# Scores of layer 1's first attention in PSUM groups of three banks instead of two

## The chip, the cores and the metric

The kernel runs on one core of a Trainium2 chip, as one launch. The metric is device time in microseconds (us) of that launch; lower is better. Engines are named as the profile names them: PE is TensorE (PEld its weight loads), ACT is ScalarE, DVE is VectorE, POOL is GpSimd, SP the queue that issues most DMAs. A PSUM bank holds 512 fp32 numbers in each of 128 partitions, and this part of the kernel uses all eight banks.

## The reference

Four layers, each an attention and a feed-forward part, on four sequences of 1024 tokens of width 128. The change touches only the first attention of layer 1. Cut to that:

```
mean = jnp.mean(sequence, axis=-1, keepdims=True)
var  = jnp.mean(jnp.square(sequence - mean), axis=-1, keepdims=True)
x = (sequence - mean) / jnp.sqrt(var + EPS) * ln_gamma + ln_beta
q = _split_heads(x @ Wq.T + bq)          # 16 heads of 8
k = _split_heads(x @ Wk.T + bk)
v = _split_heads(x @ Wv.T + bv)
scores = jnp.einsum('bhqd,bhkd->bhqk', q, k) / scale
scores = jax.nn.sigmoid(scores - mu) * jnp.exp(scores)
scores = scores / jnp.sum(scores, axis=-1, keepdims=True)
out = jnp.einsum('bhqk,bhkd->bhqd', scores, v)
return out @ Wo.T + bo
```

Every score therefore goes through ScalarE twice, once as sigmoid and once as exp, and through VectorE once, for their product. The sum over keys comes out of the value product itself, since a column of ones stands beside the values.

## The kernel before

`_attention1` (line 652) works through 16 pairs n of a sequence b and a group g of four heads. The queries of a pair are taken in two halves of 512 (`qh`), so that the stage has 32 equal **halves**. Keys lie on the partitions, 128 at a time (`kc`, 0 to 7), queries on the free axis. The four heads of a group lie on partitions 0, 32, 64 and 96 of the query and key tiles, so the score matmuls of four heads use four different row strips of TensorE. One score tile of one head and one block of keys, 128 keys by 512 queries, is one bank; a half has 32 of them, here called **units**.

A half is made of two **passes** over the same 32 units, because sigmoid and exp need different tables in ScalarE:

- In the first pass (x from 0 to 7) PE computes the scores of two units (line 723) into a `big` PSUM tile of two banks, and one ACTIVATE over 128 x 1024 numbers (line 734) turns them into a tile `p` in SBUF.
- In the second pass (x from 8 to 15) PE computes the same scores again, one ACTIVATE with the other function (line 738) makes a tile `e`, and VectorE multiplies `p` by `e` in place (line 740).

The order of the two functions alternates from half to half (`turn`), so that one table load per half is enough. Sigmoid takes its bias from a column in SBUF (`neg_mu`), exp takes a constant.

`weigh` is the value product of one block of keys: four matmuls (line 418, in `_weigh`), one per head, that add to the one-bank tile `av`. They are put into a list `waiting` and taken out of it by hand: one per x, only while x is below `LAG` = 3 or from 8 + `LAG` on. So blocks 0 to 4 are weighed at x = 11 to 15, and blocks 5 to 7 at x = 0 to 2 of the next half. After block 7 VectorE copies `av` out (line 757) and hands `_normalise` (four transposes into the bank `misc`, a reciprocal and a product) to the background work.

Background work is a queue of generators, `later`, of which one step is taken at every x, after the two groups of that x. Besides `_normalise` it holds `_project_out` (for each sequence two rounds of four transposes, line 449, and one output matmul, line 455), and `prepare`, which makes queries, keys and values of the next sequence while the present one is worked on. It is added at the first half of g = 1, three times in all. Its 17 steps are: a load; four times a projection (PE matmul line 376, VectorE line 378, then ScalarE line 388 one step later, then VectorE line 390 and the DMAs to DRAM one step later); four times two value matmuls (line 408) and one VectorE addition (line 411). Projection and value matmuls take their PSUM tiles from the same `big` pool as the scores, in the same rotation.

The engines PE, DVE and ACT run in program order here (`manual_schedule`): an instruction that waits holds up all that stand behind it on its engine. The buffers are: `big` three tiles of two banks, `misc` and `av` one bank each, `p` 18 tiles of 1024 numbers, `e` four.

Of the kernel before, what the change touches and what calls it, by code (L numbers as in the profile page):

```python
# [10 lines left out]
F32 = mybir.dt.float32  # L11
# [208 lines left out]
def _bc(ap, axis, n):  # L220

    ap = ap.unsqueeze(axis)
    shape = list(ap.shape)
    shape[axis] = n
    return ap.to_broadcast(shape)
# [139 lines left out]
def _project_halves(k, wts, biases, rotary, xin, hl, ps, w, adder=None):  # L365

    nc = k.nc
    for part in range(2):  # L370
        for h in range(2):
            own = slice(h * W, (h + 1) * W)
            x = w.tile([P, W], F32, name="px")
            t = ps()
            for n, wt in enumerate(wts[part]):
                nc.tensor.matmul(t[:, n, :], wt, xin[:, own], start=True, stop=True)
            if rotary is None:
                nc.vector.tensor_scalar(x, t[:, 0, :], biases[part][0], None, ALU.add)
            else:
                r = [w.tile([P, W], F32, name=f"rot{n}") for n in range(2)]  # L380
                for n in range(2):
                    nc.vector.scalar_tensor_tensor(
                        r[n], t[:, n, :], biases[part][n], rotary[:, n, own], ALU.add, ALU.mult
                    )
                adder.tensor_tensor(x, r[0], r[1], ALU.add)
            yield
            hi, lo = w.tile([P, W], R, name="phi"), w.tile([P, W], R, name="plo")
            nc.scalar.copy(hi, x)
            yield
            nc.vector.tensor_tensor(lo, x, hi.bitcast(F32), ALU.subtract)  # L390
            for n in range(4):
                half = (lo if n // 2 else hi) if part == 0 else (lo if n % 2 else hi)
                nc.sync.dma_start(hl[part][:, n, :, own], half.bitcast(F32))
            yield
# [7 lines left out]
def _values(k, xin, wv, bv, v, ps):  # L402

    nc = k.nc
    for t in range(0, 8, 2):
        vp = ps()
        for m in range(2):
            nc.tensor.matmul(
                vp[:, m, :VW], xin[:, (t + m) * P : (t + m + 1) * P], wv, start=True, stop=True
            )  # L410
        nc.vector.tensor_tensor(v[:, t : t + 2, :], vp[:, :, :VW], _bc(bv, 1, 2), ALU.add)
        yield
# [239 lines left out]
def _attention1(k, a):  # L652
    nc, tc = k.nc, k.tc
    LAG = 3
    with ExitStack() as s:
        pool = lambda name, bufs, **kw: s.enter_context(tc.tile_pool(name=name, bufs=bufs, **kw))
        wp = pool("w1", 1)
        wqk, wv, wo = k.load(wp, a["l1_wqk"]), k.load(wp, a["l1_wv"]), k.load(wp, a["l1_wo"])
        bv = wp.tile([P, VW], F32, name="bv1")
        nc.sync.dma_start(bv, a["l1_bv"].to_broadcast([P, VW]))  # L660
        neg_mu = wp.tile([P, 1], F32, name="neg_mu")
        nc.vector.tensor_scalar(neg_mu, k.vec("l1_mu"), -1.0, None, ALU.mult)
        wts = [[wqk[:, m * P : (m + 1) * P]] for m in range(2)]
        biases = [[k.vec("l1_b" + x)] for x in "qk"]
        xp, vp, op, w = pool("xl", 1), pool("v", 2), pool("o", 2), pool("aw", 2)
        hp, pp, ep = pool("heads", 2), pool("p", 18), pool("e", 4)
        big = pool("big", 3, space=PSUM)
        misc = pool("misc", 1, space=PSUM)
        avp = pool("av", 1, space=PSUM)
        two = lambda: big.tile([P, 2, W], F32, name="big")  # L670
        one = lambda: misc.tile([P, W], F32, name="misc")
        heads, values = {}, {}

        def prepare(b):
            xl = xp.tile([P, L], F32, name="xl")
            nc.sync.dma_start(xl, k.xl[b])
            values[b] = vp.tile([P, 8, VW], F32, name="v")
            yield
            yield from _project_halves(k, wts, biases, None, xl, k.hl[b], two, w)
            yield from _values(k, xl, wv, bv, values[b], two)  # L680

        def load(n):
            q, key = hp.tile([P, L], R, name="q32"), hp.tile([P, L], R, name="k32")
            for part, dst in ((1, key), (0, q)):
                src = _to_heads(k.hl[n // 4][part], n % 4)
                nc.sync.dma_start(dst.bitcast(F32), src.rearrange("h r t -> (h r) t"))
            heads[n] = q, key

        scale = 8.0**-0.5
        funcs = [(AF.Sigmoid, neg_mu), (AF.Exp, 0.0)]  # L690
        later = _Steps()
        for _ in prepare(0):
            pass
        load(0)
        s.enter_context(tc.manual_schedule(engines=ENGINES))
        o = None
        turn = 0
        waiting = []
        for n in range(16):
            b, g = divmod(n, 4)  # L700
            if g == 0:
                o = op.tile([P, 8, D], F32, name="o")
            if g == 1 and b + 1 < B:
                ready = prepare(b + 1)
                later.add(ready)
            if g == 3 and b + 1 < B:
                later.until(ready)
            if n + 1 < 16:
                load(n + 1)
            q, key = heads.pop(n)  # L710
            v = values[b]
            for qh in range(2):


                first = {}
                av = None
                for x in range(16):
                    kc = x % 8
                    for pair in range(2):
                        ps = two()  # L720
                        for jj in range(2):
                            rows = slice(32 * (2 * pair + jj), 32 * (2 * pair + jj) + 32)
                            nc.tensor.matmul(  # L723
                                ps[:, jj, :],
                                key[rows, kc * P : (kc + 1) * P],
                                q[rows, qh * W : (qh + 1) * W],
                                start=True,
                                stop=True,
                                tile_position=(32 * (2 * pair + jj), 0),
                            )  # L730
                        f, bias = funcs[turn]
                        if x < 8:
                            p = pp.tile([P, 2, W], F32, name="p")
                            nc.scalar.activation(p, ps, f, bias=bias, scale=scale)  # L734
                            first[kc, pair] = p
                        else:
                            e = ep.tile([P, 2, W], F32, name="e")
                            nc.scalar.activation(e, ps, f, bias=bias, scale=scale)  # L738
                            p = first[kc, pair]
                            nc.vector.tensor_tensor(p, p, e, ALU.mult)  # L740
                        if pair == 0 and waiting and (x < LAG or x >= 8 + LAG):
                            waiting.pop(0)()
                    later.step()
                    if x == 7:
                        turn ^= 1
                    if x < 8:
                        continue
                    if av is None:
                        av = avp.tile([P, W], F32, name="av")

                    def weigh(av=av, v=v, b=b, g=g, qh=qh, kc=kc, first=first, o=o):
                        pts = [first[kc, j // 2][:, j % 2, :] for j in range(4)]
                        _weigh(k, v, g, kc, pts, av, slice(0, W))
                        if kc < 7:
                            return
                        osb = w.tile([P, W], F32, name="osb")
                        nc.vector.tensor_copy(osb, av)
                        later.add(_normalise(k, osb, o[:, 4 * qh : 4 * qh + 4], g, one, w))
                        if g == 3 and qh == 1:
                            copy = nc.vector.tensor_copy  # L760
                            later.add(
                                _project_out(k, b, o, wo, k.vec("l1_bo"), k.x, one, w, copy)
                            )

                    waiting.append(weigh)
        while waiting:
            waiting.pop(0)()
        later.finish()


# [1451 lines left out]
```

## Time and profile before

| what | value |
|---|---|
| median of 3 runs | 4753.9 us (4752.63 to 4770.15) |
| the profiled execution's own time | 4760.07 us |
| its span | 4758.3 us |
| mean granted clock of PE in it | 0.862 |
| first score matmul and last `weigh` of the stage | 1376.4 us and 2483.3 us from the span's start |
| ACT busy over the span | 2562.6 us (54%) |
| PE busy over the span | 3887.6 us (82%) |
| DVE busy over the span | 3111.6 us (65%) |
| ACT busy from 1378 to 2486 us | 1047.59 of 1108 us |
| DVE busy there | 654.56 us |
| PE busy there, and its granted clock | 938.82 us, 0.74 |

The profile is one execution. Its page lists busy time per engine, then the span in 40 slices of 119 us with the busy share of each engine in tenths, then DMA, the chain of work that ended last, and groups of instructions by source line, with their count, busy time, mean duration and the idle time of the engine just before them. A view by time merges runs of equal instructions: start, length, engine, line, what it writes and reads, the count, and in square brackets the idle time before it and who ended it. A mean duration is longer than the time from one start to the next, since ACT and DVE begin an instruction before the last one's write is acknowledged.

### The profile page before, as it was taken

To read this page: it belongs to the slowest core of one execution; us is meant where nothing else is said; L and a number is where in the kernel's file an instruction comes from. 1 tells how busy PE (TensorE), PEld (TensorE's weight loads), DVE (VectorE), ACT (ScalarE), POOL (GpSimd) and SP (SyncE) were. 2 spreads that over 40 slices of the span, in tenths; PEclk is the share of its full clock that TensorE was granted. 3 is DMA by queue.
4 is the path that set the end of the run, shared out by engine and by line. 5 is a ranking of instruction groups with operands and counts; after the bars stand their busy time and mean duration, and the time that the engine had idled before them with its cause. 6 is when DMAs were issued, how large, how long until landed. Compare 5 with 4: busy or idle time off the path is not lost. (4 is left out here: it accounts for less than half of the span.)

```text
span 4758.3 us, 54361 instructions
## 1 busy us (share of the span) xinstructions
PE 3887.6 (82%) x20924; PEld 1774.2 (37%) x20924; DVE 3111.6 (65%) x4404; ACT 2562.6 (54%) x3611; POOL 649.7 (14%) x639
## 2 busy tenths in 40 slices
PE   4679999998968888888877888888879966888564
PEld 3223333364332222222224555555534543333221
DVE  5868989722336656565657888888465323899876
ACT  1257877831259999999984555455422112344331
POOL 1310000003100000000003232233103122000132
PEclk6689999999967777777778999999889987999788
DMA  2411121021221010100002111111100223300001
GB/s 86 118 41 55 29 59 26 11 72 49 14 83 58 18 49 18 36 27 18 18 13 65 36 41 35 40 34 32 37 0 23 63 64 83 97 0 9 0 0 53
DMA packets 107494, 191.81 MB, mean 40 GB/s; under 512 B 23138, under 2 KB 48354, under 8 KB 105378
## 3 DMA queue, kind: packets, MB, share of 16 engines
q1 hardware_dynamic: 98756, 166.31, 12.3%
q0 software_dynamic: 8192, 16.79, 1.7%
q10 hardware_dynamic: 288, 5.24, 0.3%
q8 instruction: 165, 2.70, 0.2%
q14 instruction: 93, 0.76, 0.1%
HBM read 95.00 MB, written 67.39 MB: 34 GB/s over the span
## 5 line engine op out<-in xcount | busy, mean ns | idle before, releaser
L740 DVE TENSOR_TENSOR p<-p,e 128x1024 f32<-128x1024 f32 x512 | 586.7, 1221 | 321.7 <-ACT e L738 321.7
L723 PE MATMUL big<-q,k 32*128 32x512 f32 x2048 | 560.3, 633 | 180.6 <-ACT p L734 74.9
L533 DVE TENSOR_REDUCE m<-mx 128x2 f32<-128x1024 f32 x512 | 620.9, 1223 | 101.4 <-PE mx L525 94.2
L418 PE MATMUL av<-p,v 128*32 128x256 f32 (+1 forms) x5632 | 666.4, 528 | 0.3
L616 ACT ACTIVATE p<-s 128x512 f32<-128x512 f32 x1024 | 550.9, 597 | 184.7 <-PE s L607 171.5
L723 PEld LDWEIGHTS big<-q,k 32*128 32x128 f32 x2048 | 210.8, 229 | 707.0 <-ACT e L738 347.3
L607 PE MATMUL s<-q,k 64*128 64x512 f32 x1024 | 277.7, 494 | 48.4 <-DMA q<-mrows 33.4
L738 ACT ACTIVATE e<-big,neg_mu 128x1024 f32<-128x1024 f32 x256 | 262.0, 1125 | 11.7 <-PE big L723 11.4
L525 PE MATMUL mx<-k,q 64*128 64x512 f32 x1024 | 238.8, 437 | 32.3 <-DVE m L533 17.8
L734 ACT ACTIVATE p<-big,neg_mu 128x1024 f32<-128x1024 f32 x256 | 261.2, 1199 | 3.0 <-PE big L723 2.8
L738 ACT ACTIVATE e<-big 128x1024 f32<-128x1024 f32 x256 | 243.0, 1040 | 28.8 <-PE big L723 27.2
L734 ACT ACTIVATE p<-big 128x1024 f32<-128x1024 f32 x256 | 239.4, 1076 | 8.2 <-PE big L723 8.1
L1177 POOL TENSOR_TENSOR lqk<-lt 128x512 f32<-128x512 f32 x128 | 162.5, 1269 | 518.1 <-DVE lt L1168 461.3
L1150 PE MATMUL lps<-f_wqkv,lh 128*128 128x512 f32 x384 | 215.2, 649 | 11.7 <-DVE lo L1305 6.8
L1871 PE MATMUL sm<-hist,in_const_sb 128*128 128x512 f32 x252 | 144.0, 701 | 93.1 <-ACT hist L1896 79.5
L1031 POOL DMA_INDIRECT cl_row<-res,back x128 | 121.2, 947 | 713.7 <-DMA in_l_su_sb<-in_l_su 474.3
L418 PEld LDWEIGHTS av<-p,v 128*32 128x32 f32 x5632 | 121.3, 111 | 253.1 <-issue 202.6
L607 PEld LDWEIGHTS s<-q,k 64*128 64x128 f32 x1024 | 107.5, 184 | 284.9 <-issue 162.3
L1268 ACT ACTIVATE lsm<-lsm 128x512 f32<-128x512 f32 x128 | 80.6, 630 | 222.1 <-DVE lsm L1267 220.7
L1896 ACT COPY hist<-sm 128x992 f32<-128x992 f32 (+1 forms) x65 | 64.9, 999 | 224.0 <-DVE pro L1879 143.4
L950 POOL DMA_INDIRECT buf<-xtok,to x128 | 125.9, 983 | 407.7 <-DMA buf<-xtok,to 221.3
L1143 POOL MEMSET lva<- 128x32 f32 x16 | 2.4, 152 | 1148.1 <-PE av L418 1148.1
(412 smaller groups left out, 6888.5 us busy)
## 6 DMA issues: line engine op xcount, KB each, us to landing
hl<-phi SPq DMA_DIRECT2D x64, 256.0 KB, 2.9
hl<-plo SPq DMA_DIRECT2D x64, 256.0 KB, 3.5
lvs<-lva SPq DMA_DIRECT2D x16, 520.0 KB, 5.7
q<-hl SPq DMA_DIRECT2D x32, 256.0 KB, 5.2
k<-hl SPq DMA_DIRECT2D x32, 256.0 KB, 5.9
q<-hl SPq DMA_DIRECT2D x16, 512.0 KB, 5.3
k<-hl SPq DMA_DIRECT2D x16, 512.0 KB, 3.5
lvs<-lva SPq DMA_DIRECT2D x16, 390.0 KB
```

The lines of the kernel that those rows point to most:

```text
L418: k.nc.tensor.matmul(av[32 * j : 32 * j + 32, cols], v[:, kc, 9 * (4 * g + j) : 9 * (4 * g + j) + 32], pts[j][:, cols], start=kc == 0, sto ...
L525: nc.tensor.matmul(ps[:, i, :], q[rows, gg, qt * P : (qt + 1) * P], key[rows, gg, half * W : (half + 1) * W], start=True, stop=True, tile_ ...
L533: nc.vector.tensor_reduce(m[:, qt, gg, :, half], ps, AX.X, ALU.max)
L607: nc.tensor.matmul(ps, key[rows, half, kc * P : (kc + 1) * P], q[rows, half, qh * W : (qh + 1) * W], start=True, stop=True, tile_position= ...
L616: nc.scalar.activation(p, ps, AF.Exp, scale=8.0**-0.5)
L723: nc.tensor.matmul(ps[:, jj, :], key[rows, kc * P : (kc + 1) * P], q[rows, qh * W : (qh + 1) * W], start=True, stop=True, tile_position=(3 ...
L734: nc.scalar.activation(p, ps, f, bias=bias, scale=scale)
L738: nc.scalar.activation(e, ps, f, bias=bias, scale=scale)
L740: nc.vector.tensor_tensor(p, p, e, ALU.mult)
L1150: nc.tensor.matmul(ps, z.h[:, t * P : (t + 1) * P], wqkv[:, own], start=True, stop=True)
L1177: nc.gpsimd.tensor_tensor(z.qk[t][:, own], r[0], r[1], ALU.add)
L1871: nc.tensor.matmul(st[:, n], w, u[:, n], start=first, stop=last)
```

## The change

Scores are grouped by three units instead of two. A half is now 22 steps x, eleven per pass: ten groups of three units and one of two. Every step has one group, with one ACTIVATE over up to 1536 numbers and, in the second pass, one product of that size. `big` becomes two tiles of three banks (still six banks), `p` 14 tiles and `e` three tiles of 1536 numbers. Projections and value matmuls use one such tile each and leave part of it empty.

The units of a group run across heads and blocks, so a block of keys can end inside a group. A `weigh` is put on the list with the number of the group that completes it, and taken out three groups later: blocks 0 to 7 are complete at x = 12, 13, 14, 16, 17, 18, 20 and 21, and weighed at x = 15, 16, 17, 19, 20, 21 and at x = 1 and 2 of the next half. A step of background work is taken at three of every four x, that is 17 instead of 16 steps per half. The instruction order of SP and POOL stays as it was.

```diff
-        hp, pp, ep = pool("heads", 2), pool("p", 18), pool("e", 4)
-        big = pool("big", 3, space=PSUM)
+        hp, pp, ep = pool("heads", 2), pool("p", 14), pool("e", 3)
+        big = pool("big", 2, space=PSUM)
-        two = lambda: big.tile([P, 2, W], F32, name="big")
+        three = lambda: big.tile([P, 3, W], F32, name="big")
...
-            yield from _project_halves(k, wts, biases, None, xl, k.hl[b], two, w)
-            yield from _values(k, xl, wv, bv, values[b], two)
+            yield from _project_halves(k, wts, biases, None, xl, k.hl[b], three, w)
+            yield from _values(k, xl, wv, bv, values[b], lambda: three()[:, :2])
...
-                for x in range(16):
-                    kc = x % 8
-                    for pair in range(2):
-                        ps = two()
...
+                for x in range(22):
+                    units = range(x % 11 * 3, min(x % 11 * 3 + 3, 32))
+                    ps = three()
+                    for u in units:
+                        kc, j = divmod(u, 4)
+                        rows = slice(32 * j, 32 * j + 32)
+                        nc.tensor.matmul(ps[:, u % 3, :], ...)
+                    m = len(units)
+                    if x < 11:
+                        p = pp.tile([P, 3, W], F32, name="p")
+                        nc.scalar.activation(p[:, :m], ps[:, :m], f, bias=bias, scale=scale)
+                        first.append(p)
+                    else:
+                        e = ep.tile([P, 3, W], F32, name="e")
+                        nc.scalar.activation(e[:, :m], ps[:, :m], f, bias=bias, scale=scale)
+                        p = first[x - 11]
+                        nc.vector.tensor_tensor(p[:, :m], p[:, :m], e[:, :m], ALU.mult)
+                    group += 1
+                    if waiting and waiting[0][0] + LAG <= group:
+                        waiting.pop(0)[1]()
+                    if x % 4 < 3:
+                        later.step()
...
-                        if pair == 0 and waiting and (x < LAG or x >= 8 + LAG):
-                            waiting.pop(0)()
-                    later.step()
...
+                    kc = (units[-1] + 1) // 4 - 1
+                    if x < 11 or kc == units[0] // 4 - 1:
+                        continue
...
-                    waiting.append(weigh)
+                    waiting.append((group, weigh))
```

More of the change, by code (lines that the diff above doesn't have):

```diff
@@ L696, in _attention1 @@
         o = None
-        turn = 0
+        turn, group = 0, 0
         waiting = []
@@ L712, in _attention1 @@
             for qh in range(2):
-                first = {}
+                first = []
                 av = None
-                for x in range(16):
-                    kc = x % 8
-                    for pair in range(2):
-                        ps = two()
[L721 to L740, printed above, removed]
-                        if pair == 0 and waiting and (x < LAG or x >= 8 + LAG):
-                            waiting.pop(0)()
-                    later.step()
-                    if x == 7:
@@ new lines, in _attention1 @@
+                for x in range(22):
[4 more added lines that the diff above has]
+                        rows = slice(32 * j, 32 * j + 32)
+                        nc.tensor.matmul(
+                            ps[:, u % 3, :],
+                            key[rows, kc * P : (kc + 1) * P],
+                            q[rows, qh * W : (qh + 1) * W],
+                            start=True,
+                            stop=True,
+                            tile_position=(32 * j, 0),
+                        )
+                    m = len(units)
+                    f, bias = funcs[turn]
+                    if x < 11:
[12 more added lines that the diff above has]
+                        later.step()
+                    if x == 10:
@@ L745, in _attention1 @@
                         turn ^= 1
-                    if x < 8:
+                    kc = (units[-1] + 1) // 4 - 1
+                    if x < 11 or kc == units[0] // 4 - 1:
                         continue
@@ L751, in weigh @@
                     def weigh(av=av, v=v, b=b, g=g, qh=qh, kc=kc, first=first, o=o):
-                        pts = [first[kc, j // 2][:, j % 2, :] for j in range(4)]
+                        pts = [first[u // 3][:, u % 3, :] for u in range(4 * kc, 4 * kc + 4)]
                         _weigh(k, v, g, kc, pts, av, slice(0, W))
@@ L763, in weigh @@
                             )
-                    waiting.append(weigh)
+                    waiting.append((group, weigh))
         while waiting:
-            waiting.pop(0)()
+            waiting.pop(0)[1]()
         later.finish()
```

## The prediction

> **What bounds the kernel now.** I read the span in slices first, to find which engine fills the stage that is changed.
>
> ```profile
> PE   4679999998968888888877888888879966888564
> DVE  5868989722336656565657888888465323899876
> ACT  1257877831259999999984555455422112344331
> PEclk6689999999967777777778999999889987999788
> ```
>
> The stage is slices 12 to 20. ACT stands at 9 and PE at 8, under a granted clock of only 0.7; DVE has room. So ScalarE is the bound, nearly always busy, with a slowed PE close behind. The groups by line give the size of its instructions and what its few waits are for.
>
> ```profile
> L740 DVE TENSOR_TENSOR p<-p,e 128x1024 f32<-128x1024 f32 x512 | 586.7, 1221 | 321.7 <-ACT e L738 321.7
> L738 ACT ACTIVATE e<-big,neg_mu 128x1024 f32<-128x1024 f32 x256 | 262.0, 1125 | 11.7 <-PE big L723 11.4
> L738 ACT ACTIVATE e<-big 128x1024 f32<-128x1024 f32 x256 | 243.0, 1040 | 28.8 <-PE big L723 27.2
> ```
>
> ACT waits for score matmuls and nothing else, in the second pass. The timeline of ACT shows how: one exp pass, one sigmoid pass.
>
> ```profile
> 1606.21 6.52 ACT L738 ACTIVATE e<-big 128x1024 f32<-128x1024 f32 x7
> 1613.46 1.94 ACT L738 ACTIVATE e<-big 128x1024 f32<-128x1024 f32 x2 [0.73 <-PE big L723]
> 1615.68 6.52 ACT L738 ACTIVATE e<-big 128x1024 f32<-128x1024 f32 x7 [0.28 <-PE big L723]
> ...
> 1638.60 7.14 ACT L738 ACTIVATE e<-big,neg_mu 128x1024 f32<-128x1024 f32 x7
> 1646.21 2.12 ACT L738 ACTIVATE e<-big,neg_mu 128x1024 f32<-128x1024 f32 x2 [0.47 <-PE big L723]
> 1648.80 7.14 ACT L738 ACTIVATE e<-big,neg_mu 128x1024 f32<-128x1024 f32 x7 [0.47 <-PE big L723]
> ```
>
> After seven groups, when `weigh` begins, ACT waits once or twice for PE: about 0.7 us per sigmoid pass and 1.1 per exp pass over the ordinary halves, mean 0.9. PE's timeline in such a pass says why.
>
> ```profile
> 1509.07 0.79 PE L723 MATMUL big<-q,k 32*128 32x512 f32 x2 [0.21 <-ACT e L738]
> 1509.79 1.94 PE L418 MATMUL av<-p,v 128*32 128x512 f32 x8
> 1511.66 0.80 PE L723 MATMUL big<-q,k 32*128 32x512 f32 x4
> 1512.38 1.94 PE L418 MATMUL av<-p,v 128*32 128x512 f32 x8
> 1514.25 0.80 PE L723 MATMUL big<-q,k 32*128 32x512 f32 x4
> 1514.98 1.55 PE L418 MATMUL av<-p,v 128*32 128x512 f32 x8
> 1516.46 0.50 PE L723 MATMUL big<-q,k 32*128 32x512 f32 x4
> 1516.90 1.07 PE L418 MATMUL av<-p,v 128*32 128x512 f32 x8
> ```
>
> The same `weigh` takes 1.94 us at first and 1.07 from the fourth on, a fill 0.80 and then 0.50: the first pass, where PE pauses 0.21 us in every group, leaves PE at a low clock, and some 6 us of unbroken work bring the high one. At the low clock a fill of four and a `weigh` take 2.60 us from start to start, against two ACTIVATEs of 1.00 or 0.92.
>
> **The change, part by part.** All in us against the profiled execution; a half is 1/32 of the stage.
>
> *A. Fewer ACTIVATEs.* Seven of sigmoid take 7.14 us, the last counted with its 1.12, so one starts 1.00 after the other; exp (6.52, last 1.03) 0.92. Exp over 512 numbers, in the attention of layer 0 (line 616), comes as two in 1.08 with one lasting 0.597: 0.49 apart. So 512 numbers cost 0.43, and the fixed part is 0.06 for exp, and 0.14 for sigmoid if its extra 0.08 is per instruction. Each pass has 11 instead of 16: 5 x 0.06 + 5 x 0.14 = 1.0 per half, **-32**. The nearest rows can't tell whether sigmoid's 0.08 is per instruction or per number; if per number, it is 5 x 0.06 x 2 = 0.6, so -19. The Trainium skill ("ScalarE: Activation LUTs", What ACT_TABLE_LOAD costs) says that a pointer operand adds about 93 ns to each instruction, which speaks for -32. A full group then takes 1.43 (sigmoid) or 1.35 (exp).
>
> *B. The slow `weigh`s meet fewer buffers.* Three tiles let PE fall behind by two groups of 0.92 to 1.00, less a fill of 0.8 and two handoffs of 0.1: slack 0.9. Two tiles leave one group, 1.43 or 1.35 less 1.0: slack 0.4. Blocks 0, 1, 2 are also weighed at three groups in a row, x = 15, 16, 17: a fill and a slow `weigh` each, 0.73 + 1.87 = 2.60, against 1.43. Step by step, sigmoid, zero where ACT starts group 14: fill 15 0.1 to 0.9; `weigh` 0 to 2.7; fill 16 to 3.5, so ACT starts 16 at 3.6 instead of 2.86, 0.74 lost. `weigh` 1 to 5.3; fill 17 to 6.1, ACT starts it at 6.2 instead of 5.03, 1.17 lost. `weigh` 2 is the third, partly at high clock, to 7.5; fill 18 to 8.0, ACT at 8.1 instead of 7.63, 0.47 lost. Together 2.4 and for exp 2.6; where the clock rises one `weigh` sooner, as in some passes of before, about 1.4. I take 2.0 against 0.9 now: +1.0 rounded down, x 29 ordinary halves, **+29**. Bounds: 0 (clock up after one `weigh`) to +46. The skill ("TensorE: Matmul & The Clock Gate", Part 1) has full clock after about 3.4 us of sustained work. By that the second `weigh` would already speed up, the loss would be about 1.0 and B about +3; this trace needs some 6 us, and I go by it.
>
> *C. Blocks 6 and 7* are weighed at x = 1 and 2 of the next half, where only slack 0.4 to 0.9 is left. At high clock fill plus `weigh` is 0.44 + 1.0 = 1.44 against 1.43: no loss; at low clock 2.60, and up to 0.6 lost beyond what before shows there (0.33 in some halves). **+6** (29 x 0.2), 0 to +17.
>
> *D. Projections and values in the rotation of two.* In before, the three halves with them last 41.9, 40.6 and 41.8 us against some 33.5: 8 more, of which four casts on ACT are 2.0 and waits nearly 6. Now such an event holds one of the only two tiles, so ACT runs dry while the other is refilled: fill 0.8 and two handoffs, 1.0; a projection at low clock (2.08 in the trace) outlasts a group by 0.6 more. Four projections: 4 x 1.4 = 5.6. Values come at x = 17, 18, 20, 21 behind DVE's product (3 x 512 / 1024 x 1.14 = 1.7): the tile is free after product 1.7 and addition 0.5, then a fill 0.5 to 0.8 and ACT 1.35: 4.3 for two groups that need 2.7. Four events, three such spans: 3 x 1.6 = 4.8, and `weigh`s of 1.0 queued between, some 1.4. In all 11.8 against 6, and B's 1.0 comes here too: 6.8 x 3, **+21**. Bounds: +6 (values lie beside DVE's lag) to +33.
>
> *E. Output projections*: four transposes and a matmul at low clock, 1.1 and 2.08, against slack 0.4 instead of 0.9. Before waits 0.60, 0.87 and 0.33 per sequence; now 1.3 more, x 3 sequences inside the stage, **+4**, -2 to +8.
>
> *Hidden.* VectorE's products lose 160 fixed parts of about 0.07 us (1.14 apart for 1024 numbers at the 0.52 to 0.53 per 512 that larger rows imply), at nothing: DVE is busy 655 of 1108 us. If it were the bound, that would be -11. DMAs and the SP and POOL queues keep their order; `prepare` ends a half before its heads are loaded. Start and end of the stage are as before.
>
> Sum: -32 + 29 + 6 + 21 + 4 = **+28**. The profiled execution took 4760.1, so 4788; it stands 6.2 over the median of the runs, so I predict **4782** for the median.
>
> **Rivals.**
> 1. *ScalarE gets its gain* (faster). If PE reaches `weigh` 0 at the high clock, B's losses go and the 0.9 of now too: B = -26, C = 0. With D at +12 and E at 0: -32 - 26 + 12 = -46, about 4708. It decides where fewer than two `weigh`s per pass last over 1.5 us. Against it: in the first pass fills are busy 0.8 of 1.4 us now, less than 0.8 of 1.0 before, and even that left the clock low.
> 2. *The stalls are small* (no change). The clock rises one `weigh` early, B = +12, and D is +12: -32 + 12 + 6 + 12 + 4 = +2, 4756. For it: passes of before with only one wait.
> 3. *VectorE through three `e` tiles* (slower still). Products of 1.67 against ACT's 1.35 to 1.43 lag by 0.24 to 0.32 per group; a `weigh` three groups behind its product instead of five then holds PE. PE already waits 47 us for products. From five groups of lag on, 0.5 to 1 more per half: +16 to +32, so 4798 to 4814.
>
> **Chances.** Forecast (+12 to +45) 0.52; rival 2 (-24 to +12) 0.24; rival 1 0.10; rival 3 0.14. A change under 0.5% (24 us) is about what a measurement of this kernel cannot tell from none. Of the forecast some 0.11 lies below +24. Faster 0.10, same 0.35, slower 0.55. The range leaves out rival 1's far half and the top of rival 3: 4738 to 4812 for the median (-16 to +58).
>
> **What would show it.** A: L735 and L739 starting 1.35 and 1.43 apart. B: ACT waits before groups 16, 17, 18 of the second pass, 1.4 to 2.6 together, under `weigh`s of 1.9. D: three halves of about 48 us. Wrong if the granted clock of the stage rises above 0.8, or if ACT waits under 1 us per ordinary half.

## The result and the profile after

The changed kernel takes **4801.7 us** (median of 4 runs, 4789.4 to 4807.83); the kernel before, on the same chip, takes 4753.26 (4 runs, 4751.58 to 4770.15). The ratio is 1.0086, 95% interval 1.0067 to 1.0105. By the interval the change costs 32 to 50 us, and the medians differ by 48; +28 was predicted, and the range reached to 4812. In all experiments below a kernel is compared with runs of the kernel before in the same series, whose median lay between 4742.64 and 4762.56.

The profiled execution after took 4800.84 us, its span 4799.1. I measure the **stage** from its first ACTIVATE of `p` to the end of its last of `e`: 1102.0 us before, 1137.4 after, **+35.4**. The other 5 us of the difference of the two profiled executions (40.7) lie outside it, within what runs of one kernel differ by. Every stage length and every wait below is that of one profiled execution. Nineteen runs of the kernel before in one series spread over 15.7 us, so a few us between the stages of two kernels show little. The span in slices after:

```profile
PE   4779999998957777777776888888879966888564
DVE  5868989623345555556567888888565323799876
ACT  1257877831258989989983555545422111344331
PEclk6689999999967767777778999999889986999788
```

In slices 12 to 20, counted from 0, PE has gone from 8 to 7, and its granted clock in one of them from 7 to 6; ACT has fallen from an even 9 to a mixture of 8 and 9. DVE still has room. The engine that bounds the stage has less to do and waits more. The groups of instructions by line say how much less, and for whom it waits (busy time, mean ns of one, idle time before it):

```profile
L741 DVE TENSOR_TENSOR p<-p,e 128x1536 f32<-128x1536 f32 (+1 forms) x352 | 578.2, 1704 | 372.7 <-ACT e L739 372.0
L739 ACT ACTIVATE e<-big,neg_mu 128x1536 f32<-128x1536 f32 (+1 forms) x176 | 251.4, 1504 | 34.7 <-PE big L723 34.5
L739 ACT ACTIVATE e<-big 128x1536 f32<-128x1536 f32 (+1 forms) x176 | 238.4, 1418 | 49.1 <-PE big L723 47.1
```

VectorE's product of 1536 numbers (1024 in one group of eleven) takes 1704 ns in the mean and waits for ACT almost alone, as before. ACT's second pass waited 11.7 and 28.8 us before (sigmoid, exp); it waits 34.7 and 49.1 now. ACT's timeline shows where, in one exp and one sigmoid pass:

```profile
1546.45 6.82 ACT L739 ACTIVATE e<-big 128x1536 f32<-128x1536 f32 x5
1554.11 1.45 ACT L739 ACTIVATE e<-big 128x1536 f32<-128x1536 f32 x1 [0.83 <-PE big L723]
1556.22 6.48 ACT L739 ACTIVATE e<-big 128x1536 f32<-128x1536 f32 x5 [0.66 <-PE big L723]
...
1579.46 7.26 ACT L739 ACTIVATE e<-big,neg_mu 128x1536 f32<-128x1536 f32 x5
1587.35 1.54 ACT L739 ACTIVATE e<-big,neg_mu 128x1536 f32<-128x1536 f32 x1 [0.63 <-PE big L723]
1589.94 1.54 ACT L739 ACTIVATE e<-big,neg_mu 128x1536 f32<-128x1536 f32 x1 [1.05 <-PE big L723]
1592.54 5.41 ACT L739 ACTIVATE e<-big,neg_mu 128x1536 f32<-128x1536 f32 x4 [1.05 <-PE big L723]
```

Five groups run without a wait, one every (6.82 - 1.45) / 4 = 1.34 us (exp) or (7.26 - 1.54) / 4 = 1.43 (sigmoid). Then ACT waits before groups 16, 17 and, in the second pass shown, 18. PE's timeline in the exp pass gives the reason:

```profile
1550.64 0.80 PE L723 MATMUL big<-q,k 32*128 32x512 f32 x3 [0.55 <-ACT e L739]
1551.36 1.97 PE L418 MATMUL av<-p,v 128*32 128x512 f32 x8
1553.26 0.80 PE L723 MATMUL big<-q,k 32*128 32x512 f32 x3
1553.99 1.75 PE L418 MATMUL av<-p,v 128*32 128x512 f32 x8
1555.67 0.50 PE L723 MATMUL big<-q,k 32*128 32x512 f32 x3
1556.10 1.06 PE L418 MATMUL av<-p,v 128*32 128x512 f32 x8
```

With the first `weigh` PE stops waiting for ACT (no bracket any more) and ACT waits for PE instead. A fill and a `weigh` take 2.6 and 2.4 us against the 1.34 of a group until the clock rises; then 1.5. In the sigmoid pass the third `weigh` is slow too, and there ACT waits three times:

```profile
1584.64 1.93 PE L418 MATMUL av<-p,v 128*32 128x512 f32 x8
1587.23 1.94 PE L418 MATMUL av<-p,v 128*32 128x512 f32 x8
1589.83 1.94 PE L418 MATMUL av<-p,v 128*32 128x512 f32 x8
1592.84 1.10 PE L418 MATMUL av<-p,v 128*32 128x512 f32 x8
```

The 32 halves, sorted by what else PE has in them (mean length; mean of ACT's waits in the first and in the second pass, us). All but 3.9 us of the waits after are for PE; the rest, 0.73 in each half with projections among it, are for VectorE.

| halves | before | after |
|---|---|---|
| 20 ordinary | 33.42; 0.06, 0.92 | 34.19; 0.31, 2.28 |
| 3 with projections and values | 41.42; 1.25, 4.27 | 48.24; 4.31, 8.21 |
| 3 after those | 34.76; 1.99, 0.75 | 34.38; 1.75, 2.32 |
| 6 with output projections | 34.18; 0.47, 0.83 | 34.30; 1.05, 1.38 |

All waits of ACT in the stage, a first one of 13.7 that both have left out, are 52.3 us before and 116.2 after: **+64**. ACT's busy time on lines 734/738 against 735/739 is 1005.5 and 974.9: **-30.6**. The two make the +35.4 but for 2 us.

### The profile page after: what moved, and what is told of

Read it like the earlier page. It is cut to its first block, busy times and chain, and to the rows that moved or that the text cites. A ratio compares the mean times of both kernels' runs of the same rounds, so it can differ in the third digit from the quotient of the medians.

```text
span 4799.1 us, 53664 instructions
## 1 busy us (share of the span) xinstructions
PE 3816.7 (80%) x20924; PEld 1735.5 (36%) x20924; DVE 3104.1 (65%) x4244; ACT 2535.4 (53%) x3291; POOL 649.0 (14%) x639
## 5 line engine op out<-in xcount | busy, mean ns | idle before, releaser
L741 DVE TENSOR_TENSOR p<-p,e 128x1536 f32<-128x1536 f32 (+1 forms) x352 | 578.2, 1704 | 372.7 <-ACT e L739 372.0
L418 PE MATMUL av<-p,v 128*32 128x256 f32 (+1 forms) x5632 | 695.6, 542 | 6.5 <-DVE p L741 6.1
L723 PE MATMUL big<-q,k 32*128 32x512 f32 x2048 | 450.5, 641 | 279.4 <-ACT p L735 149.3
L723 PEld LDWEIGHTS big<-q,k 32*128 32x128 f32 x2048 | 166.9, 233 | 742.9 <-ACT e L739 313.3
L739 ACT ACTIVATE e<-big,neg_mu 128x1536 f32<-128x1536 f32 (+1 forms) x176 | 251.4, 1504 | 34.7 <-PE big L723 34.5
L739 ACT ACTIVATE e<-big 128x1536 f32<-128x1536 f32 (+1 forms) x176 | 238.4, 1418 | 49.1 <-PE big L723 47.1
L735 ACT ACTIVATE p<-big,neg_mu 128x1536 f32<-128x1536 f32 (+1 forms) x176 | 250.5, 1515 | 17.5 <-PE big L723 17.5
L735 ACT ACTIVATE p<-big 128x1536 f32<-128x1536 f32 (+1 forms) x176 | 234.7, 1435 | 13.8 <-PE big L723 13.3
```

The source lines that it names most:

```text
L418: k.nc.tensor.matmul(av[32 * j : 32 * j + 32, cols], v[:, kc, 9 * (4 * g + j) : 9 * (4 * g + j) + 32], pts[j][:, cols], start=kc == 0, sto ...
L723: nc.tensor.matmul(ps[:, u % 3, :], key[rows, kc * P : (kc + 1) * P], q[rows, qh * W : (qh + 1) * W], start=True, stop=True, tile_position ...
L735: nc.scalar.activation(p[:, :m], ps[:, :m], f, bias=bias, scale=scale)
L739: nc.scalar.activation(e[:, :m], ps[:, :m], f, bias=bias, scale=scale)
L741: nc.vector.tensor_tensor(p[:, :m], p[:, :m], e[:, :m], ALU.mult)
```

## Experiments

The theory was that of the prediction: the gain on ScalarE is real, and slow `weigh`s at a low clock spend it, because two tiles leave PE one group of slack. The rivals: VectorE's products hold PE through `weigh`s three groups behind (rival 3), or the order of PE's instructions rather than the depth of the tiles does it.

**1. Projections and values out of the rotation.** They take one-bank tiles of `misc`.

```diff
-            yield from _project_halves(k, wts, biases, None, xl, k.hl[b], three, w)
-            yield from _values(k, xl, wv, bv, values[b], lambda: three()[:, :2])
+            yield from _project_halves(k, wts, biases, None, xl, k.hl[b], lambda: one()[:, None, :], w)
+            yield from _values(k, xl, wv, bv, values[b], lambda: one()[:, :2*VW].rearrange(...))
```

> The changed kernel, with projections and value matmuls of the next sequence taking their PSUM tile from the one-bank pool misc instead of the rotation of two big tiles. Theory (two tiles leave PE one group of slack, and a projection that holds one of them lets ScalarE run dry): the three halves with projections, now 47.1, 50.3 and 47.4 us, fall to 42 to 44; the other halves stay at 34.2; together -12 to -20 us against the changed kernel's 4802. Rival (VectorE's products, three groups behind, hold PE): the products and additions stay where they are, so these halves lose at most 2 us each, -6 in all.

Measured: 4766.71 against 4742.64, ratio 1.0045 (1.003 to 1.0059); stage 1121.3. The halves with projections fell from 48.24 only to 46.52, a miss: with one bank for the values, PE waits in each for VectorE's addition before it (3.4 us at the longest), and ACT then once for 4.2 us. Of the 16 us that the stage is shorter, these halves give 5, those after them 4, and the ordinary ones, which the edit doesn't touch, 7. The rotation is a part of D's price, but `misc` is no free place for values.

**2. Two more groups between product and `weigh`.**

```diff
-    LAG = 3
+    LAG = 5
```

> The changed kernel with LAG = 5: each value product comes five groups after the group that completes its block, instead of three. Rival (products lag behind and hold PE): PE's waits for products, 57 us now, fall under 15, and ScalarE's waits in the second pass of ordinary halves, 2.28 us now, fall by 0.5 to 1: -16 to -30 us. Theory (slow value products in consecutive groups against one group of slack): they come as close together as before, at x = 17, 18, 19, still at the low clock, so the waits stay at 2.0 to 2.5 and only move two groups later; -5 to +5 us.

Measured: 4761.66 against 4742.64, ratio 1.0034 (1.0022 to 1.0047); stage 1123.4, that is -14. By the ratios, 1.0086 and 1.0034, it is some 25 us. PE's waits for products at line 418 (us in total, times, longest), after and then in this run:

```profile
PEld av L418 <- DVE p L741: 50.5, 76, 1.5
PE av L418 <- DVE p L741: 6.1, 14, 0.6
```

```profile
PEld av L418 <- DVE p L741: 2.9, 6, 1.0
```

So rival 3 has a part that I had put at near nothing: some 10 of the 14 us come in the three halves with projections (48.24 to 44.99), 7 in the ordinary ones (34.19 to 33.85), and halves with output projections give 2.5 back. But the second pass of the ordinary halves still waits 1.97 us, 1.60 of it for PE and 0.37 for VectorE's products: the waits for PE that remain have another cause.

**3. The kernel before with two tiles.**

```diff
-        big = pool("big", 3, space=PSUM)
+        big = pool("big", 2, space=PSUM)
```

> The kernel before, groups of two banks and its order of value products untouched, but two big tiles instead of three. Theory: the slack falls from 0.9 us to about zero (one group of 0.92 to 1.00 less a fill of 0.8 and two handoffs), so ScalarE's waits in ordinary halves rise from 0.98 to 2 or more, partly in the first pass as well, and the three halves with projections grow by 4 or more: +40 to +80 us against 4753. Rival (it is the order of the value products, three in consecutive groups, that costs, and not the number of tiles): waits as before, +0 to +10, but for the three projection halves, +6 to +12.

Measured: 4841.71 against 4742.64, ratio 1.0196 (1.0176 to 1.0217); stage 1202.5, +100, more than the 80 expected at most. The order of before, with one tile less, waits 2.11 in the second pass of an ordinary half, about what the change does. Two tiles alone are enough to make such waits, without the new order. That the order adds nothing isn't shown, since the slack by the prediction's count is smaller here (about zero, against 0.4 in the changed kernel).

**4. PE kept busy ahead of the `weigh`s.** Matmuls of 192 to 512 columns into `av`, which the first `weigh` overwrites.

```diff
+    fillers = {9: 192, 10: 192, 11: 192, 12: 512, 13: 256, 14: 256}
...
+                    if x in fillers:
+                        if av is None:
+                            av = avp.tile([P, W], F32, name="av")
+                        nc.tensor.matmul(av[:, : fillers[x]], k.ident, k.xn[:, : fillers[x]], start=True, stop=True)
```

> The changed kernel with six extra matmuls per half, over 192 to 512 columns of constant data into the value tile before its first real use (the first real product overwrites it), after the fills of x = 9 to 14: they fill PE's pauses ahead of the value products, 1.9 us at the pass boundary among them. Nothing of the result changes. Theory (the slow clock at the first value products makes the waits): all value products last about 1.07 us, ScalarE's second-pass waits in ordinary halves fall from 2.28 us to under 0.6, less up to 0.4 that the fillers cost: -35 to -55 us, the stage's granted clock from 0.72 to over 0.82. Rival (VectorE's lag or the order): the waits stay over 1.5 and move to PE's waits for products; -10 us or nothing, or slower by the fillers.

Measured: 4795.81 against 4742.64, ratio 1.0103 (1.0085 to 1.0121), stage 1157.7. The view by windows shows why (the window, its length, busy time of PE, PEld, DVE, ACT and POOL with counts in brackets, the granted clock, DMA share and GB/s):

```profile
1544.00:1550.00 6.00, 6.00 (x18) 2.32 (x15) 5.12 (x3) 4.92 (x4) 0.00 (x0) 0.50 0.00 0
1550.00:1555.00 5.00, 5.00 (x25) 0.80 (x25) 3.92 (x4) 3.06 (x3) 0.00 (x0) 0.50 0.01 3
1555.00:1560.00 5.00, 4.67 (x34) 1.29 (x36) 4.09 (x3) 3.85 (x3) 0.00 (x0) 0.85 0.00 0
```

PE is busy without a pause for 11 us at a granted clock of 0.50: the expectation that this would raise the clock missed. The first `weigh`s stay slow (1.94), so this run neither helps the kernel nor decides between the theories.

**5. The high clock forced.** Three matmuls of 512 columns, back to back, right before the first `weigh`.

```diff
+                    if x == 14:
+                        for _ in range(3):
+                            nc.tensor.matmul(av, k.ident, k.xn[:, :W], start=True, stop=True)
```

> The changed kernel with three full 512-column matmuls of constant data into the value tile straight after the fill of x = 14, ahead of the first value product, which overwrites them. The fillers of e4 left the clock low: 192 to 512 columns each between fills, with a drain after each. These three follow each other without a pause. They cost about 6 us at the low clock, so ScalarE must wait some 4 to 5 us once, at group 15 or 16; that wait is the price and says nothing. What tells: theory (the low clock at the first value products makes the waits at groups 16, 17 and 18): all value products after them last 1.07 us, and the later waits of the pass, 1.05 + 1.05 or 1.14 + 1.14 now, are gone (under 0.3 together). Rival (order of the products or VectorE's lag): value products are fast but waits of 0.6 or more stay at groups 17 and 18. If the first products still take 1.94 us after 6 us of matmuls, the clock follows something else than PE's recent work.

Measured, in a single run: 4840.69 us against 4762.56, stage 1185.8. The total only shows the price of the three. The timelines of PE and of ACT answer the question:

```profile
1553.21 5.49 PE L734 MATMUL av<-xn,in_const_sb 128*128 128x512 f32 x6
...
1559.24 1.06 PE L418 MATMUL av<-p,v 128*32 128x512 f32 x8
...
1560.67 1.07 PE L418 MATMUL av<-p,v 128*32 128x512 f32 x8
```

```profile
1549.64 5.48 ACT L742 ACTIVATE e<-big 128x1536 f32<-128x1536 f32 x4
1559.36 9.37 ACT L742 ACTIVATE e<-big 128x1536 f32<-128x1536 f32 x7 [4.24 <-PE big L723]
```

The first three `weigh`s now take 1.06 or 1.07 instead of 1.97, 1.75 and 1.06 (none of the others in this pass over 1.32), and after the one wait of 4.24 that pays for the three matmuls ACT runs seven groups without any. The same holds in all 29 halves without projections: the first three `weigh`s take 1.06 or 1.07, and ACT has that one wait in the second pass and no other. VectorE's lag isn't what went away, for PE waits for products no less than in the changed kernel:

```profile
PEld av L418 <- DVE p L744: 53.7, 62, 1.5
PE av L418 <- DVE p L744: 16.3, 30, 0.6
```

With PE at the high clock, one group of slack is enough: B's waits are the low clock's.

**6 to 9. Blocks 6 and 7 kept back.** The idea was a longer unbroken stretch of PE: the last two `weigh`s of a half move from the start of the next half to its second pass, ahead of its own. In the changed kernel:

```diff
-                    if waiting and waiting[0][0] + LAG <= group:
+                    if x >= 11 and waiting and waiting[0][0] + LAG <= group:
```

> The changed kernel with the value products of blocks 6 and 7 held back from x = 1 and 2 of the next half to x = 11 and 12, the pass boundary, where PE has a pause of 1.97 us under ScalarE's table load. Theory: two slow products move out of the slack of 0.4 into a pause, and they raise the clock for the first products of the second pass: first-pass waits 0.3 fall to 0, second-pass waits from 2.28 to 1.0 to 1.6: -20 to -35 us against the changed kernel, so a ratio to the kernel before of 1.001 to 1.004. Rival (VectorE's lag): the products come long after VectorE is done with them either way, so nothing moves, -5 to +5 us.

Measured: 4858.65 against 4762.56, ratio 1.02 (1.0177 to 1.0224), stage 1190.5. The same in the kernel before, with 20 tiles `p` to hold the products for so long (`waiting` holds the half beside each `weigh`):

```diff
-        hp, pp, ep = pool("heads", 2), pool("p", 18), pool("e", 4)
+        hp, pp, ep = pool("heads", 2), pool("p", 20), pool("e", 4)
...
-                        if pair == 0 and waiting and (x < LAG or x >= 8 + LAG):
-                            waiting.pop(0)()
+                        held = x in (8, 9) and waiting and waiting[0][0] != (n, qh)
+                        if pair == 0 and waiting and (x < 1 or held or x >= 8 + LAG):
+                            waiting.pop(0)[1]()
```

> The kernel before with the same idea: blocks 6 and 7 of a half are weighed at x = 8 and 9 of the next half instead of x = 1 and 2, with 20 tiles for p instead of 18. Theory: its waits of 0.98 us in ordinary halves come from the same slow products, so they fall to 0.2 to 0.6, and those after a projection half fall too: -10 to -25 us, ratio 0.995 to 0.998. Rival: with a slack of 0.9 the boundary is no better a place, -3 to +5 us.

Measured: 4823.74 against 4762.56, ratio 1.0128 (1.0089 to 1.0167), stage 1168.9. Both miss, for a cause that I hadn't counted. PE's waits in the first of them:

```profile
PE misc L435 <- DVE osb L762: 55.4, 26, 2.7
```

Its weight loads at that line wait another 66 us, partly at the same time. The transposes of `_normalise` come one background step after block 7, and wait for VectorE's copy of `av`, which in a second pass stands behind products. So I moved them seven background steps on, first in the changed kernel, then in the one before:

```diff
-    yield
+    for _ in range(steps):
+        yield
...
-                        later.add(_normalise(k, osb, o[:, 4 * qh : 4 * qh + 4], g, one, w))
+                        later.add(_normalise(k, osb, o[:, 4 * qh : 4 * qh + 4], g, one, w, 7))
```

> e6 with its new wait taken away: the value products of blocks 6 and 7 stay at x = 11 and 12, and the transposes that read the copied-out result come seven background steps after the copy instead of one, that is at the start of the next half. In e6 they stood in PE's queue behind a copy that VectorE takes up only after its products, and held PE for 2.7 us. Theory: PE's waits for that copy, 131 us in e6, fall under 10; what is left of the second-pass waits in ordinary halves, 3.7 in e6 and 2.3 in the changed kernel, is 0.9 to 1.5; -15 to -35 us against the changed kernel, ratio to the kernel before 1.001 to 1.005. Rival (the pass boundary is a bad place in itself, since a slow product there delays the fills of x = 12 to 14): waits stay at 2 or more, ratio 1.008 or above.

Measured: 4800.66 against 4760.07, ratio 1.0077 (1.0061 to 1.0094), stage 1148.7.

> e7 with the same repair: the kernel before, blocks 6 and 7 weighed at x = 8 and 9 of the next half, the transposes seven steps after the copy. Theory: waits of ordinary halves, 0.98 in the kernel before and 2.7 in e7, fall to 0.2 to 0.7: ratio 0.995 to 1.000. Rival (the boundary is a bad place in itself): waits above 1.2, ratio above 1.002.

Measured: 4783.81 against 4760.07, ratio 1.0043 (1.003 to 1.0056), stage 1120.2. Those waits went, but the waits at the `weigh`s didn't. In ordinary halves the changed kernel's second pass now waits 1.79 instead of 2.28, but its first pass 0.78 instead of 0.31; in the kernel before the second pass waits 1.28 instead of 0.92. In these runs the start of a half is no worse a place for blocks 6 and 7 than its middle.

**10. Both cures.** LAG = 5, and the projections alone (not the values) in `misc`.

```diff
-    LAG = 3
+    LAG = 5
...
-            yield from _project_halves(k, wts, biases, None, xl, k.hl[b], three, w)
+            yield from _project_halves(k, wts, biases, None, xl, k.hl[b], lambda: one()[:, None, :], w)
```

> The changed kernel with LAG = 5 as in e2 and the projections alone (not the values) in the one-bank pool misc. e1 showed that values in one bank make PE wait 4.2 us for VectorE, e2 that products five groups behind spare the projection halves 3 us. Theory: the two first-pass waits per projection half that are 1.4 each go to 0.7, so these halves, 45.0 in e2, come to 42 to 44, and the others stay at 33.9: -3 to -9 us against e2, ratio 1.002 to 1.003. Rival (the low clock alone sets these waits, 2.08 us per projection, wherever its tile lies): no change, ratio 1.0034.

Measured: 4769.52 (10 runs) against 4760.07 (19 runs), ratio 1.0015 (1.0005 to 1.0024); stage 1109.1, halves with projections 43.2. It is the best version with groups of three, and still not faster than groups of two: ordinary halves stay at 33.92 against 33.42, with 1.95 us of second-pass waits. Against run 2 the stage is 14.3 shorter: 5.4 in the halves with projections, 3.8 in those after, and 6.6 in halves with output projections, which the edit doesn't touch, while the ordinary halves are 1.6 longer; those 6.6 I can't explain. By the ratios run 10 is only some 9 us faster than run 2.

**11 and 12. Almost no `weigh`s.** The value products of blocks 0 to 6 are left out, so the output is not that of the reference; block 7's four matmuls stay in each half. `True` makes block 7 start its sum anew. Once with groups of three, once with groups of two:

```diff
-                        _weigh(k, v, g, kc, pts, av, slice(0, W))
                         if kc < 7:
                             return
+                        _weigh(k, v, g, kc, pts, av, slice(0, W), True)
```

> The changed kernel with the value products of blocks 0 to 6 left out: in each half only block 7 is weighed (four matmuls instead of 32), so the output is not that of the reference. PE then has in the second pass what it has in the first, and every other instruction stays. Theory (the gain on ScalarE is real and is given back because the weighs meet one tile of slack at the low clock, plus the projections): ordinary halves last 31.4 to 31.8 us (34.19 less the waits of 0.31 and 2.28), with under 0.5 of waits in the second pass; halves with projections still last 44 or more. Against its counterpart with groups of two the stage is then 0 to 25 us shorter (-30 for fewer ACTIVATEs, +12 to +20 for the three halves with projections, at a clock that may be lower than now). Rival (the second-pass waits have another source, VectorE's products or the hand-over of two tiles as such): ordinary halves stay over 33, and the stage is longer than the counterpart's.

> The kernel before with the same value products, those of blocks 0 to 6, left out, so the output is not that of the reference: the counterpart with groups of two and three tiles. Theory: ordinary halves last 32.4 to 32.7 us (33.42 less waits of 0.06 and 0.92), that is 0.7 to 1.2 longer than the counterpart with groups of three, where the full kernels stand 0.8 the other way; halves with projections stay near 41; the stage is some 1065 to 1075. Rival: ordinary halves are not longer than those of the counterpart with groups of three.

Measured: 4799.36 and 4793.75 against 4759.28, ratios 1.0085 (1.0069 to 1.0102) and 1.0079 (1.0062 to 1.0096). The stages are 1136.6 and 1130.5. With 28 of 32 value matmuls per half gone, the one kernel is no shorter and the other is 28 us *longer*. The windows over the whole stage, of the kernel before and then of run 12, show how:

```profile
1378.00:2486.00 1108.00, 938.82 (x4326) 292.63 (x4326) 654.56 (x655) 1047.59 (x1069) 0.93 (x4) 0.74 0.08 26
```

```profile
1378.00:2510.00 1132.00, 885.54 (x2524) 321.65 (x2524) 645.65 (x647) 1046.28 (x1066) 0.00 (x0) 0.53 0.08 27
```

The granted clock falls from 0.74 to 0.53 (0.54 in run 11). With the `weigh`s in, the clock is higher. The second pass is as the theory had it: 0.00 us of waits in ordinary halves with groups of two; 0.52 with groups of three, of a new kind. But at the start of the next half block 7 now takes up to 3.06 us in both (2.40 or 2.79 in most halves with groups of two, 3.02 to 3.06 with groups of three), and ACT waits there 1.15 and 1.73. A `weigh` at the low clock takes 1.94; the rest comes with PE's waits for VectorE's products (weight loads 28 us in all with groups of two, 46 with three). So the lengths (33.98 and 34.11) missed what I expected of both, and the rivals' signs came true to the letter, halves over 33 us and a stage longer than the counterpart's, though not for their cause, waits in the second pass. Without their waits they are 32.83 and 31.86: the 0.97 of A is there. In run 11 ACT's timeline shows both kinds:

```profile
1535.48 11.14 ACT L735 ACTIVATE p<-big,neg_mu 128x1536 f32<-128x1536 f32 x8 [1.47 <-PE big L723]
...
1556.27 1.45 ACT L739 ACTIVATE e<-big 128x1536 f32<-128x1536 f32 x1 [0.17 <-DVE p L741]
1557.94 1.45 ACT L739 ACTIVATE e<-big 128x1536 f32<-128x1536 f32 x1 [0.22 <-DVE p L741]
```

The first is PE's single late `weigh`. The second is VectorE: three `e` tiles let ACT run ahead until it is held to one product, 1.67 us from start to start against its own 1.34. In the exp passes of run 11, that is the next bound behind PE.

## Why the prediction came out right, step by step

Waits are measured as the sums over halves of the table above.

| step | predicted, us | measured, us |
|---|---|---|
| A, fewer ACTIVATEs | -32 | -30.6 |
| B, second-pass waits outside the three halves with projections | +29 | +35.1 |
| C, blocks 6 and 7: first-pass waits, ordinary halves and those after projections | +6 | +4.4 |
| D, halves with projections and values: waits | +21 | +21.0 |
| E, output projections: first-pass waits | +4 | +3.5 |
| sum | +28 | +33.4 |

The sum is that of the stage (35.4 measured there). The median of all runs stands 48 above that of the kernel before, and 41 by the ratio, so the forecast of 4782 was some 13 to 20 us low; 5 us of the 41 between the profiled executions lie outside the stage, where the prediction had nothing.

- **A** held: 1.43 and 1.34 from start to start, as worked out from rows of 512 and 1024 numbers. Sigmoid's extra 0.08 us is per instruction.
- **B** was the right mechanism, and the term that was mis-sized. I worked out 2.4 and 2.6 for passes in which the clock rises in the third `weigh`, 1.4 where it rises one sooner, and took 2.0. The third wait was put at 0.47, with the third `weigh` partly at the high clock. Where it comes, it is 1.05 or 1.14, as long as the second, since the third `weigh` is slow to its end (1.94): in 13 of the 29 halves (all 13 without output projections) the clock rises 8.3 to 8.8 us after the first `weigh` starts, where I had read some 6 from the kernel before (there it comes after 2.9 to 6.2 in the same 23 halves). These passes wait 2.7 (sigmoid) or 3.1 (exp). In the ten other halves without output projections it rises after 4.1 to 4.8 us, the third `weigh` takes 1.06 or 1.07, and the waits sum to 1.5 to 1.7. The mean of ordinary halves is 2.28 where I took 2.0. Run 5 shows that the low clock causes the waits, run 3 that two tiles are enough to let it, runs 11 and 12 that without the `weigh`s PE's lateness leaves the second pass.
- The clock's behaviour: in the trace after, PE is busy 4.00 of 4.00 us from 1551 to 1555 at a granted clock of 0.50, and the clock has a mean of 0.96 in the 5 us that follow. The Trainium skill ("TensorE: Matmul & The Clock Gate", Part 1) says that the window over which activity is measured, some 3.4 us, runs freely, so the number of slow matmuls varies from run to run; that agrees with two lengths of wait in otherwise equal halves, and with the records of the granted clock: in the stage after, its 65 changes all stand whole multiples of 3.413 us apart. Its rule that a window of sustained work brings full speed does not hold by the profile's busy time: run 4 has 11 us of it at 0.50. The measurement decides here, and what activity the gate counts no run separates.
- **C** held in sum, though no longer as I told it: block 6's `weigh` takes 1.87 to 2.71 us in these halves, and run 2 shows that a part of the waits is the wait for VectorE's products.
- **D** held to the microsecond as a sum, which is partly luck: each half waits 12.5 us where I worked out 11.8, and 5.5 before where I took 6. The trace of such a half shows PE's projection and what ACT waits after it:

```profile
1456.51 2.07 PE L376 MATMUL big<-xl,in_l_wqk_sb 128*128 128x512 f32 x2 [0.93 <-ACT p L735]
1458.51 1.71 PE L723 MATMUL big<-q,k 32*128 32x512 f32 x6
```

```profile
1459.35 1.54 ACT L735 ACTIVATE p<-big,neg_mu 128x1536 f32<-128x1536 f32 x1 [1.47 <-PE big L723]
...
1475.79 1.45 ACT L739 ACTIVATE e<-big 128x1536 f32<-128x1536 f32 x1 [1.56 <-PE big L723]
```

  A projection costs 1.4 to 1.6, as the step said (1.0 and 0.6). But run 2, where 3.2 us of each such half go with the products' lag alone, shows that a part of the 12.5 was no matter of the rotation; I had that part under rival 3 and not in D's 11.8.
- **Hidden** work stayed hidden: DVE's busy time from 1378 us to some 5 us past the stage's end fell by 8.1 us (654.6 to 646.5), and DVE is still busy for little more than half of the stage.
- **Rival 1** fell on its own condition: in all passes but three, two or more of the first three `weigh`s last over 1.5 us (1.97 and 1.75 above). **Rival 2**'s early rise happened in the ten halves whose waits sum to 1.5 to 1.7, too few for its total. **Rival 3** had a real part (run 2: 14 us of the stage), where I treated it as an alternative to the forecast.

Of the +35.4, 14.0 go with lag 3 and 14.3 more with the projections' place, if runs 2 and 10 are taken in that order; 7.1 stay in the best version. By the ratios it is 41, of which 25, 9 and 7. The two orders agree, the shares don't, so the split is rough. What no run separated: how much of the last is clock phase, which changes from kernel to kernel, how much depth, and how much the order of three `weigh`s in consecutive groups. Three tiles of three banks weren't tried: with `misc` and `av` they make eleven banks, and both kernels use eight.

## What to carry to other kernels

- A merged instruction saves its fixed part only where the producer keeps up. Count the slack of the PSUM rotation in microseconds of the consumer, (tiles - 1) groups less one fill and its handoffs, and set it against the longest piece of work that stands between two fills *at the clock of that moment*: here 0.4 us against 1.97.
- Fewer, larger buffers charge every foreign user of the rotation a whole tile; where that can be done give these their own bank (run 10 did it for the projections; in run 1 the values in one bank waited for VectorE), and let the consumers of a slower engine's results lie further behind.
- Removing PE work can slow a kernel: look at the granted clock of the stage before and after.

## What the runs showed of the hardware that I had not expected

- Leaving out 7/8 of the value products dropped the stage's granted clock from 0.74 to 0.53 and made the stage 28 us longer with groups of two.
- PE's busy time does not foretell the clock. In run 4 score matmuls in turn with fillers of 256 and 512 columns and the first two `weigh`s kept PE busy for 11 us at 0.50; in run 5 three back-to-back matmuls of 512 columns (5.49 us) had it high before the first `weigh`, and its mean was 0.90 from 1558 to 1563 us. What work it follows instead no run shows.
- The granted clock changes on a fixed grid: in the stage before and in the stage after all 65 changes stand whole multiples of 3.413 us from each other. Counted from the start of the first `weigh`, the rise comes in the changed kernel after 4.1 to 4.8 us in some halves and after 8.3 to 8.8 in others.
- In run 12 PE filled 11 groups in 10 us, busy 8.72 of 10.00, and the clock stayed at 0.50.
